# Output parts moved on ScalarE, X^T parts queued behind them, and W loaded elsewhere in a fused long-convolution and score kernel

## The chip, the cores and the metric

The kernel runs on one core of one Trainium2 chip. A core has a matrix engine (TensorE, PE in the profile; its weight loads, which overlap the matmuls, are PEld), three engines for elementwise work (VectorE or DVE, ScalarE or ACT, GpSimd or POOL), and a queue engine (SyncE or SP), which issues the transfers between the device's memory and the core's on-chip memory. Sixteen DMA engines carry out all transfers. The metric is the device time of one execution in microseconds (us); less is better.

## The reference

The input x has 4 images of 64 channels of 256 x 256. Two layers follow. The first filters every channel with a kernel of its own: `k = hx[i] * hy[j]`, an outer product of two vectors that a small network with sines makes, so the two-dimensional convolution is two one-dimensional ones.

```python
y = irfft2(rfft2(x, 512 x 512) * rfft2(k) / 512)[:256, :256]
x = y + x * bias[channel]
```

The second layer weighs each image's matrix of row products, adds the sum of each row to the row, and normalizes each channel over all images:

```python
scores = einsum('bpsd,bptd->bpst', x, x) / sqrt(256)
y = x + sum(scores * weights, axis=-1, keepdims=True)
y_hat = (y - mean(y)) * rsqrt(var(y) + 1e-5)     # over images, rows, columns
out = y_hat * gamma + beta
```

## The kernel before, in words

Everything is float32. The kernel goes through the 64 channels one by one; all four images of a channel are worked on together, as two pairs v = 0, 1. Each convolution is a product with a Toeplitz matrix, which is read from a table in device memory with overlapping rows. A channel passes through several stages, and different stages of different channels overlap. One turn c of the main loop (L545 to L592) contains:

- On TensorE, always in this order: `conv_x0(c)` (L233), the second convolution of channel c; `conv_z(c + 1)` (L210), the first one of the next channel; `gram(c, 0)` and `gram(c, 1)` (L270), the row products of the two pairs. This text calls one such turn on TensorE a block, and its phase is the time since its first conv_x0 matmul.
- On VectorE: `x0` (L240), which takes the convolution's result out of the accumulators and adds x times bias; `weigh` and `spread` (L290, L294, L304), which multiply the row products by W; `add_red` (L326), which adds the row sums to x0 of channel p = c - 1; and five small instructions of `scale_shift` (L386 to L394).
- On GpSimd: `all_sum` (L312), a sum over partitions of 1,024 columns, and two short sums (L330, L372).
- On ScalarE: `copy_h(c + 1)` (L192) doubles the Toeplitz rows of the next channel, which conv_z(c + 1) needs; `minus_mean` and `squares` (L361, L362, L366) of channel q = c - 2; `copy_z` (L219), four copies out of accumulators for the next block's conv_x0; `pick_red` (L319), which moves half of the row sums and which add_red waits for; `root` (L378 to L382), three tiny instructions; and four output parts.

An output part is `finish(g, sh, v, n)` (L399): ScalarE computes x0 times g plus sh for half n of pair v (L406, 128 x 512 elements), and SyncE writes the result o out (L407, 256 KB). The four parts of a channel are written (0,0), (0,1), (1,0), (1,1) in this text. Parts (0,0) and (0,1) of channel f = c - 3 come at the end of turn c; parts (1,0) and (1,1) follow in the next turn, where the channel is called e = c - 4.

The order on each engine is the order in which the program is written (`manual_schedule`, L83): nothing reorders it. All loads of the loop and all writes stand on SyncE's one queue, also in written order. An entry that has to wait holds up those behind it. A turn loads X^T of channel c + 3 in four parts of 256 KB (L72, four buffers for each pair), W of channel c + 1 (L78, 320 KB, two buffers), and the Toeplitz rows of channel c + 2 in four groups of 36 KB (L187, three buffers). Before the change a turn's queue on SyncE is: W; rows 0; part (1,0); rows 1; X^T (0,0); part (1,1); rows 2; X^T (1,0); part (0,0); rows 3; X^T (0,1); part (0,1); X^T (1,1). W's load waits until VectorE has used the W of channel c - 1 for the last time (L294).

The last two channels are written out on their own (`last_channels`, L439). It takes over the open output parts of the loop.

Of the kernel before, what the change touches and what calls it, by code (L numbers as in the profile page):

```python
# [15 lines left out]
B, C, S = 4, 64, 256  # L16
# [21 lines left out]
def conv_scores_bn_kernel(  # L38
# [29 lines left out]
    def load_xt(c, v, n):  # L68
        if not n:
            xts[c, v] = ld.tile([P, 4, S], F32, tag=f"xt{v}", name=f"xt_{c}_{v}", bufs=4)  # L70
        part = bass.ts(n, 2)
        nc.sync.dma_start(xts[c, v][:, part], xT[c, v, :, part])  # L72
# [3 lines left out]
    def load_w(c):  # L76
        w = ld.tile([P, 10, H], F32, tag="w", name=f"w_{c}", bufs=2)
        nc.sync.dma_start(w, wl[c])  # L78
        ws[c] = w
# [97 lines left out]
    def load_h(c, n):  # L177


        if not n:  # L180
            hs[c] = ld.tile([P, 2, GW], F32, tag="toep", name=f"toep_{c}")
        src = bass.AP(
            g_dram.tensor, g_dram.offset + c * 2 * GW + 16 * n,
            [[4 + C * 2 * GW, COPIES], [1, 4], [1, GW + S]],
        )
        rows = hs[c][bass.ts(n, 16)].rearrange("p a r -> p (a r)")
        nc.sync.dma_start(rows[:, : GW + S], src)  # L187

    def copy_h(c):

        toep = hs[c]
        nc.scalar.copy(toep[H:, :, :S], toep[:H, :, :S])  # L192
# [7 lines left out]
    def conv_z(c, m):  # L200


        toep = hs[c]
        p1 = [ps.tile([P, 2, S], F32, tag="ps", name=f"p1_{c}_{m}_{u}") for u in range(2)]
        for k in range(2):
            for i in range(4):
                for t in range(4):
                    u, v = t % 2, t // 2
                    rows = bass.ts(u, H)
                    nc.tensor.matmul(  # L210
                        p1[u][bass.ts(v, H), k, : S - H * i],
                        lhsT=xts[c, v][rows, i, bass.ts(2 * m + k, H)],
                        rhs=toep[rows, 1, H * i : S], start=(i == 0), stop=(i == 3),
                    )
        return p1

    def copy_z(c, m, p1):
        for u in range(2):
            nc.scalar.copy(zs[c][:, u, bass.ts(m, 2), :], p1[u][:, :, ::-1])  # L219

    def conv_x0(c, z, parts=range(2)):


        xt = [xts[c, v] for v in range(2)]
        toep, x0 = hs[c], st8[c][0]
        for m in parts:
            p2 = [ps.tile([P, 2, S], F32, tag="ps", name=f"p2_{c}_{m}_{v}") for v in range(2)]
            for i in range(2):
                for k in range(4):
                    for t in range(4):  # L230
                        v, u = t % 2, t // 2
                        rows = bass.ts(v, H)
                        nc.tensor.matmul(  # L233
                            p2[v][bass.ts(u, H), i, : S - H * k],
                            lhsT=z[rows, u, k, bass.ts(2 * m + i, H)],
                            rhs=toep[rows, 0, H * k : S], start=(k == 0), stop=(k == 3),
                        )
            for v in range(2):
                part = bass.ts(m, 2)
                nc.vector.scalar_tensor_tensor(  # L240
                    x0[:, v, part], xt[v][:, part], chan_sb[:, 0, c : c + 1],
                    p2[v][:, :, ::-1], ALU.mult, ALU.add,
                )
# [195 lines left out]
    def last_channels(c):  # L439


        p, q, f, e = c - 1, c - 2, c - 3, c - 4


        begin(p)
        copy_h(c)
        conv_x0(p, zs.pop(p))
        load_w(c)
        minus_mean(moms[f])
        squares(f, moms[f], 0)  # L450
        finish(*fins[e - 1], 1, 0)
        squares(f, moms[f], 1)
        tot = sum_squares(f, moms[f])
        fins[e] = (e, *scale_shift(e, moms[e], *scales[e]))
        begin_z(c)
        copy_z(c, 0, conv_z(c, 0))
        finish(*fins[e - 1], 1, 1)
        mom_q = sm.tile([P, 8], F32, tag="mom", name=f"mom_{q}")
        rps = [red_by_pe(q, v) for v in range(2)]
        for v in range(2):  # L460
            add_red_of(q, v, rps[v], mom_q)
        nc.gpsimd.partition_all_reduce(mom_q[:, 2:4], mom_q[:, 0:2], P, RED.add)
        scales[f] = root(f, tot)
        copy_z(c, 1, conv_z(c, 1))
        finish(*fins[e], 0, 0)
        finish(*fins[e], 0, 1)
        fins[f] = (f, *scale_shift(f, moms[f], *scales[f]))
        gram(p, 0)


        begin(c)
        minus_mean(mom_q)
        squares(q, mom_q, 0)
        squares(q, mom_q, 1)
        tot = sum_squares(q, mom_q)
        z = zs.pop(c)
        conv_x0(c, z, [0])
        mom_p = sm.tile([P, 8], F32, tag="mom", name=f"mom_{p}")
        add_red_of(p, 0, red_by_pe(p, 0), mom_p)
        conv_x0(c, z, [1])  # L480
        finish(*fins[e], 1, 0)
        finish(*fins[e], 1, 1)
        scales[q] = root(q, tot)
        fins[q] = (q, *scale_shift(q, mom_q, *scales[q]))
        finish(*fins[f], 0, 0)
        finish(*fins[f], 0, 1)
        first_mean(mom_p)
        squares(p, mom_p, 0)
        gram(p, 1)
        finish(*fins[f], 1, 0)  # L490
        finish(*fins[f], 1, 1)
        for n in range(2):
            finish(*fins[q], 0, n)
        gram(c, 0, weighed=False)
        rp = red_by_pe(p, 1)
        for u in range(2):
            weigh(c, u, banks.pop(0))
        add_red_of(p, 1, rp, mom_p)
        sums_p = sum_second(p, mom_p)
        squares(p, mom_p, 1)  # L500
        nc.gpsimd.partition_all_reduce(sums_p[:, 2:4], mom_p[:, 6:8], P, RED.add)
        for n in range(2):
            finish(*fins[q], 1, n)
        gram(c, 1, weighed=False)
        mom = sm.tile([P, 8], F32, tag="mom", name=f"mom_{c}")
        add_red_of(c, 0, red_by_pe(c, 0), mom)
        first_mean(mom)
        for u in range(2):
            weigh(c, 2 + u, banks.pop(0))
        rp = red_by_pe(c, 1)  # L510
        drift(mom_p, sums_p)
        scales[p] = root_of_rest(p, sums_p)
        add_red_of(c, 1, rp, mom)
        sums = sum_second(c, mom)
        squares(c, mom, 0)
        squares(c, mom, 1)
        nc.gpsimd.partition_all_reduce(sums[:, 2:4], mom[:, 6:8], P, RED.add)
        fins[p] = (p, *scale_shift(p, mom_p, *scales[p]))
        drift(mom, sums)
        finish(*fins[p], 0, 0)  # L520
        finish(*fins[p], 0, 1, vector=True)
        scales[c] = root_of_rest(c, sums)
        finish(*fins[p], 1, 0)
        finish(*fins[p], 1, 1)
        fins[c] = (c, *scale_shift(c, mom, *scales[c]))
        for v in range(2):
            finish(*fins[c], v, 0)
            finish(*fins[c], v, 1, vector=True)
# [16 lines left out]
    for c in range(C - 2):  # L545
        p, q, f, e = c - 1, c - 2, c - 3, c - 4
        begin(c)
        copy_h(c + 1)
        conv_x0(c, zs.pop(c))

        load_w(c + 1)
        load_h(c + 2, 0)
        if q >= 0:
            minus_mean(moms[q])
            squares(q, moms[q], 0)
        if e >= 0:
            finish(*fins[e], 1, 0)
        load_h(c + 2, 1)
        if c + 3 < C:
            load_xt(c + 3, 0, 0)  # L560
        if q >= 0:
            squares(q, moms[q], 1)
            tot = sum_squares(q, moms[q])
        if f >= 0:
            fins[f] = (f, *scale_shift(f, moms.pop(f), *scales.pop(f)))
        begin_z(c + 1)
        copy_z(c + 1, 0, conv_z(c + 1, 0))
        if e >= 0:
            finish(*fins.pop(e), 1, 1)
        load_h(c + 2, 2)  # L570
        if c + 3 < C:
            load_xt(c + 3, 1, 0)
        copy_z(c + 1, 1, conv_z(c + 1, 1))
        if f >= 0:
            finish(*fins[f], 0, 0)
        load_h(c + 2, 3)
        if c + 3 < C:
            load_xt(c + 3, 0, 1)
        if p >= 0:
            pick_red(p)  # L580
        if q >= 0:
            scales[q] = root(q, tot)
        if f >= 0:
            finish(*fins[f], 0, 1)
        if c + 3 < C:
            load_xt(c + 3, 1, 1)
        gram(c, 0)
        if p >= 0:
            moms[p] = add_red(p)
        gram(c, 1)  # L590
        if c < BY_PE:
            all_sum(c)  # L592
    last_channels(C - 1)


# [67 lines left out]
```

## Time and profile before

| What | Value |
|---|---|
| Time, median of 3 runs | 881.24 us (880.01 to 884.09) |
| Profiled execution, its own time | 883.99 us |
| Span of that execution | 882.2 us |
| Granted TensorE clock, mean | 0.992 |
| TensorE busy | 860.4 us, 98% |
| VectorE busy | 754.9 us, 86% |
| ScalarE busy | 616.7 us, 70% |
| GpSimd busy | 425.1 us, 48% |
| Moved by DMA | 169.68 MB, mean 192 GB/s |

A row of the groups in the profile gives the line, the engine, the operation, what it writes and reads, and then the busy time and the mean of one instruction. Rows of waits read "engine line waited for: us in total, times, longest us". An arrow points at what ended the wait; "issue" stands there where the engine waited for nothing that the profile shows. A row of the timeline gives start, duration, engine, line and, in brackets, the engine's idle time just before it. Start times count from the span's start. q1 is the DMA queue of SyncE; q8 carries packets of instructions for the engines.

### The profile page before, as it was taken

What the parts mean: (1) busy time and instruction counts of PE and PEld (TensorE: products, weight loads), DVE (VectorE), ACT (ScalarE), POOL (GpSimd) and SP (SyncE); (2) the same over time, 40 slices, a digit from 0 to 9 for tenths busy, and PEclk for the clock granted to TensorE, in tenths of its full rate; (3) what the DMA queues carried; (4) which work ended last, traced back from release to release, by engine and by line L of the source; (5) the groups of instructions that cost most, each with busy time, mean ns of one, the idle gap of its engine ahead of it and who ended that gap; (6) DMA issues with size and microseconds to landing.
All of it is one profiled execution on the core that took longest, in us unless ns stands there. A gap on an engine that the chain in (4) does not pass through costs nothing.

```text
span 882.2 us, 55900 instructions
## 1 busy us (share of the span) xinstructions
PE 860.4 (98%) x24678; PEld 827.0 (94%) x24678; DVE 754.9 (86%) x2642; ACT 616.7 (70%) x1212; POOL 425.1 (48%) x195
## 2 busy tenths in 40 slices
PE   7999999999999999999999999999999999999993
PEld 5999999999999999999999999999999999999992
DVE  3588988998898898898898898898898898898885
ACT  2257767767777777776776776776776776776784
POOL 0236446546545545645645644645645545645600
PEclk9999999999999999999999999999999999999996
DMA  6525556556556556556556565556556556556534
GB/s 187 178 88 176 198 197 211 198 190 212 198 196 212 192 199 208 197 194 211 192 199 209 197 197 202 196 193 207 191 192 210 183 201 206 201 193 206 182 124 169
DMA packets 89913, 169.68 MB, mean 192 GB/s; under 512 B 10566, under 2 KB 11784, under 8 KB 89672
## 3 DMA queue, kind: packets, MB, share of 16 engines
q1 hardware_dynamic: 89116, 165.51, 55.5%
q8 instruction: 194, 3.18, 1.5%
q10 hardware_dynamic: 556, 0.61, 0.2%
q14 instruction: 47, 0.39, 0.1%
HBM read 98.18 MB, written 67.76 MB: 188 GB/s over the span
## 4 chain that ended last, share of the span: by engine, by line
PE 97%; DVE 1%; ACT 0%; issue 0%; DMA 0%; ACTq 0%; SPq 0%; DVEq 0%
PE p L210 32%; PE p L233 32%; PE g L270 32%; PE rp L341 0%; PE rp L346 0%; PE idle L167 0%; DVE x L355 0%; DMA fb_sb<-in_fb 0%; ACT o L406 0%; PE ph L147 0%; PE ph L131 0%; DVE fa L134 0%; DVE fa L139 0%; DVE junk L290 0%; ACT z L219 0%
## 5 line engine op out<-in xcount | busy, mean ns | idle before, releaser
L312 POOL PARTITION_ALL_REDUCE rd<-sp x61 | 373.5, 6122 | 183.8 <-DVE sp L304 183.8
L233 PE MATMUL p<-toep,z 64*64 64x256 f32 (+3 forms) x8192 | 300.6, 296 | 1.2 <-issue 1.0
L210 PE MATMUL p<-toep,xt 64*64 64x256 f32 (+3 forms) x8192 | 299.8, 296 | 0.4 <-issue 0.2
L233 PEld LDWEIGHTS p<-toep,z 64*64 64x64 f32 x8192 | 285.5, 133 | 14.4 <-issue 2.8
L270 PE MATMUL g<-x 64*64 64x192 f32 (+1 forms) x8192 | 298.1, 296 | 0.4 <-issue 0.3
L210 PEld LDWEIGHTS p<-toep,xt 64*64 64x64 f32 x8192 | 282.9, 133 | 12.2 <-PE idle L167 0.7
L270 PEld LDWEIGHTS g<-x 64*64 64x64 f32 x8192 | 283.3, 133 | 2.8 <-issue 1.0
L290 DVE SCALAR_TENSOR_TENSOR junk<-g,w 128x192 f32<-128x192 f32 x512 | 161.1, 352 | 86.5 <-PE g L270 86.5
L406 ACT ACTIVATE o<-x,sh,g 128x512 f32<-128x512 f32 x253 | 203.5, 808 | 0.0
L240 DVE SCALAR_TENSOR_TENSOR x<-xt,chan_sb,p 128x512 f32<-128x512 f32 x256 | 174.1, 742 | 9.0 <-PE p L233 9.0
L219 ACT COPY z<-p 128x512 f32<-128x512 f32 x256 | 134.7, 577 | 31.1 <-PE p L210 31.1
L366 ACT ACTIVATE sq<-x,mom 128x1024 f32<-128x1024 f32 x128 | 146.3, 1143 | 5.4 <-DVE x L355 2.0
L326 DVE SCALAR_TENSOR_TENSOR x<-x,rd 128x1024 f32<-128x1024 f32 x122 | 144.2, 1220 | 0.1
L304 DVE SCALAR_TENSOR_TENSOR sp<-eye_sb,red,pr 128x128 f32<-128x128 f32 x488 | 138.1, 346 | 0.0
L330 POOL PARTITION_ALL_REDUCE mom<-mom x61 | 24.3, 399 | 235.0 <-DVE x L326 230.9
L294 DVE SCALAR_TENSOR_TENSOR pr<-g,w 128x256 f32<-128x256 f32 x256 | 107.5, 420 | 0.0
L319 ACT COPY rd<-rd 64x512 f32<-64x512 f32 x61 | 37.6, 616 | 91.1 <-POOL rd L312 91.1
L361 ACT ACTIVATE mom<-mom 128x1 f32<-128x1 f32 x62 | 18.3, 295 | 77.3 <-POOL mom L330 77.3
L192 ACT COPY toep<-toep 64x512 f32<-64x512 f32 x63 | 38.9, 617 | 39.9 <-DMA toep<-g_dram 26.4
L290 DVE DVE_READ_ACCUMULATOR junk<-g,w 128x1 f32 x512 | 42.6, 83 | 0.0
L372 POOL PARTITION_ALL_REDUCE tot<-mom x62 | 29.7, 480 | 9.5 <-ACT sq L366 9.5
L366 ACT ACTIVATION_READ_ACCUMULATOR sq<-x,mom 128x1 f32 x128 | 23.8, 186 | 0.0
(60 smaller groups left out, 212.0 us busy)
## 6 DMA issues: line engine op xcount, KB each, us to landing
xt<-in_xT SPq DMA_DIRECT2D x256, 256.0 KB
out<-o SPq DMA_DIRECT2D x256, 256.0 KB
w<-in_wl SPq DMA_DIRECT2D x64, 320.0 KB
toep<-g_dram SPq DMA_DIRECT2D x252, 36.0 KB
g_dram<-g_sb SPq DMA_DIRECT2D x1, 320.0 KB
g_dram<-g_sb ACTq DMA_DIRECT2D x1, 320.0 KB
decay_sb<-in_decay SPq DMA_DIRECT2D x1, 256.0 KB
fw_sb<-in_fw ACTq DMA_DIRECT2D x1, 192.0 KB
```

Source lines behind the costliest of these rows:

```text
L210: nc.tensor.matmul(p1[u][bass.ts(v, H), k, : S - H * i], lhsT=xts[c, v][rows, i, bass.ts(2 * m + k, H)], rhs=toep[rows, 1, H * i : S], sta ...
L219: nc.scalar.copy(zs[c][:, u, bass.ts(m, 2), :], p1[u][:, :, ::-1])
L233: nc.tensor.matmul(p2[v][bass.ts(u, H), i, : S - H * k], lhsT=z[rows, u, k, bass.ts(2 * m + i, H)], rhs=toep[rows, 0, H * k : S], start=(k ...
L240: nc.vector.scalar_tensor_tensor(x0[:, v, part], xt[v][:, part], chan_sb[:, 0, c : c + 1], p2[v][:, :, ::-1], ALU.mult, ALU.add,)
L270: nc.tensor.matmul(gs[u][bass.ts(h, H), o, :], lhsT=xb[rows, v, i, m, :], rhs=xb[rows, v, i, t, :], start=(i == 0), stop=(i == 3),)
L290: nc.vector.scalar_tensor_tensor(junk, g[:, part, :], 1.0 / math.sqrt(S), w[:, 3 * n : 3 * n + 3, :], ALU.mult, ALU.mult, accum_out=red0[: ...
L294: nc.vector.scalar_tensor_tensor(pr[:, b].rearrange("p (t s) -> p t s", s=H), g[:, COL, :], 1.0 / math.sqrt(S), w[:, 6:10, :], ALU.mult, A ...
L304: nc.vector.scalar_tensor_tensor(sp[:, b, part], eye_sb, red0[:, b, n : n + 1], pr[:, b, part], ALU.mult, ALU.add,)
L312: nc.gpsimd.partition_all_reduce(rd.rearrange("p b s -> p (b s)"), sp.rearrange("p b s -> p (b s)"), P, RED.add)
L326: nc.vector.scalar_tensor_tensor(x0[:, v], x0[:, v], 1.0, rd[:, 2 * v, None, :].to_broadcast([P, 4, S]), ALU.mult, ALU.add, accum_out=mom[ ...
L366: nc.scalar.activation(sq, st8[c][0][:, v], AF.Square, bias=mom[:, 5:6], accum_out=mom[:, 6 + v : 7 + v])
L406: nc.scalar.activation(o, y, AF.Identity, bias=sh, scale=g)
```

## The change

The amount of work is unchanged; every instruction and every transfer of before is there after. Moved are:

- `pick_red(p)` on ScalarE from behind part (0,0) to ahead of it.
- Part (0,1) of the output from the end of a turn to the next turn, behind `copy_h`. In the last channels the open part (0,1) of channel 58 goes to the same place.
- On SyncE's queue, the X^T parts: each now follows an output part. X^T (0,0) goes ahead of rows 1, X^T (0,1) follows part (0,0) directly, and the last one, X^T (1,1), goes with part (0,1) into the next turn, where it is loaded for channel c + 2.
- W of channel c + 1 from the head of the queue to behind X^T (1,0), ahead of rows 3.

A turn's queue on SyncE after the change is: part (0,1); X^T (1,1); rows 0; part (1,0); X^T (0,0); rows 1; part (1,1); rows 2; X^T (1,0); W; rows 3; part (0,0); X^T (0,1).

```diff
@@ last_channels
         begin(p)
         copy_h(c)
+        finish(*fins[e - 1], 0, 1)
         conv_x0(p, zs.pop(p))
         load_w(c)
@@ main loop
         begin(c)
         copy_h(c + 1)
+        if e >= 0:
+            finish(*fins[e], 0, 1)
+        if c + 2 < C and c:
+            load_xt(c + 2, 1, 1)
+        load_h(c + 2, 0)
         conv_x0(c, zs.pop(c))
-
-        load_w(c + 1)
-        load_h(c + 2, 0)
         if q >= 0:
             minus_mean(moms[q])
             squares(q, moms[q], 0)
         if e >= 0:
             finish(*fins[e], 1, 0)
-        load_h(c + 2, 1)
         if c + 3 < C:
             load_xt(c + 3, 0, 0)
+        load_h(c + 2, 1)
         if q >= 0:
             squares(q, moms[q], 1)
             tot = sum_squares(q, moms[q])
...
         load_h(c + 2, 2)
         if c + 3 < C:
             load_xt(c + 3, 1, 0)
+        load_w(c + 1)
+        load_h(c + 2, 3)
         copy_z(c + 1, 1, conv_z(c + 1, 1))
+        if p >= 0:
+            pick_red(p)
         if f >= 0:
             finish(*fins[f], 0, 0)
-        load_h(c + 2, 3)
         if c + 3 < C:
             load_xt(c + 3, 0, 1)
-        if p >= 0:
-            pick_red(p)
         if q >= 0:
             scales[q] = root(q, tot)
-        if f >= 0:
-            finish(*fins[f], 0, 1)
-        if c + 3 < C:
-            load_xt(c + 3, 1, 1)
         gram(c, 0)
```

## The prediction

> **What bounds the kernel now.** I read the page first (busy shares, then the chain that ended last), then the waits, then one block on ScalarE and SyncE in the timeline.
>
> ```profile
> span 882.2 us, 55900 instructions
> ...
> PE 860.4 (98%) x24678; PEld 827.0 (94%) x24678; DVE 754.9 (86%) x2642; ACT 616.7 (70%) x1212; POOL 425.1 (48%) x195
> ...
> q8 instruction: 194, 3.18, 1.5%
> ```
>
> TensorE is busy for 98% of the span, and 97% of the chain of waits lies on it. The stretch 16.7 to 850.7 us of the loop has 831.99 us of TensorE in 834.00. The chain shows the three parts of a channel, L233 (conv_x0), L210 (conv_z) and L270 (gram), with 4.36, 4.37 and 4.35 us. A channel's block thus takes 13.08 us, and most blocks take exactly that. Next, the waits of the engines and of the DMA queue:
>
> ```profile
> ACT rd L319 <- POOL rd L312: 91.1, 60, 2.3
> ...
> ACT mom L361 <- POOL mom L330: 77.3, 60, 5.6
> ...
> ACT toep L192 <- DMA toep<-g_dram: 26.4, 34, 2.4
> ACT toep L192 <- issue: 13.2, 19, 1.7
> ...
> PEld p L233 <- issue: 2.8, 6, 1.1
> ...
> PEld g L270 <- issue: 1.0, 3, 0.4
> ```
>
> ScalarE waits in three places of a block, together (91.1 + 77.3 + 26.4 + 13.2)/60 = 3.5 us, and none of them holds up TensorE. SyncE's queue waits 169.1 us in 62 times for VectorE before it can load W, and 202.9 us for output parts. TensorE's only loop waits are of kind "issue": nothing in the program releases them. The chain shows one, the largest:
>
> ```profile
> 679.92 1.64 PE p L233 x32
> 681.56 0.71 issue
> 682.27 1.75 PE p L233 x27
> ```
>
> From the starts of the L233 groups I took the length of every block. After the first, eleven loop blocks exceed 13.08 us, and their excess sums to 4.8 us. The weight load after each gap above 0.25 us stands at the same place of TensorE's instruction stream, counted modulo 256, and an instruction packet (queue q8, 194 of them, 16 KB each) ends 1.3 to 1.5 us before it. So these are waits for instructions. Laying packet k beside the time at which TensorE passed the boundary before it shows that each is asked for one boundary ahead, 4.36 us early. From request to end it takes 2.04 us in the mean. It stalls TensorE when that passes about 4.36 - 1.35 = 3.0 us. That happens when data fill the DMA engines: requests at 10.5 to 11.5 us of a block, behind the long burst of transfers, take 2.7 to 3.1 us in the mean, those at 5.0 to 5.5, in the pause, 1.4.
>
> [...]
>
> **The change, part by part.** I lay block 441.54 to 454.62 out anew (phases count from its start; a phase over 13.08 belongs to the next block).
>
> ```profile
> 440.87 0.61 ACT L319 COPY rd<-rd 64x512 f32<-64x512 f32 x1 [1.57 <-POOL rd L312]
> ...
> 442.22 0.80 ACT L406 ACTIVATE o<-x,sh,g 128x512 f32<-128x512 f32 x1
> 443.79 0.62 ACT L192 COPY toep<-toep 64x512 f32<-64x512 f32 x1 [0.77 <-issue]
> 445.40 0.29 ACT L361 ACTIVATE mom<-mom 128x1 f32<-128x1 f32 x1 [0.99 <-POOL mom L330]
> ```
>
> *pick_red ahead of part (0,0).* It waits for GpSimd's sum, which ends at 440.9 whatever ScalarE does, so it starts when it did; its idle time grows from 1.57 to 2.37. Queued behind it: part (0,0), root and copy_h. Part (0,0) (0.80) and root (0.74) end at 441.48 + 1.54 = 443.02, where root and part (0,1) ended before: copy_h can start as early as it did. VectorE's add_red takes pick_red's result at 442.43, as before. Root is 0.8 later, at 443.0; VectorE reads it at 450.18. Cost 0. Were GpSimd late, all five would be late as they were before.
>
> *Part (0,1) behind copy_h.* copy_h waits for its fourth row group until 443.79 and ends at 444.41. The part runs to 445.21, in the idle 0.99 us before 445.40. Cover left: 0.19 us. Where copy_h is later (2.8 us into the block at worst, against 2.25 here), the part pushes the squares by up to 0.4 us, then the copies of z; those end at phase 10.0 and TensorE wants them at 13.08. Cost 0; without that 3 us it would be 0.4 us in some blocks. In the last channels one part moves the same way, in the same cover.
>
> *W.* It leaves the place where it blocked SyncE from phase 1.9 to 5.06 and goes behind the third X^T part, issued at about 10.8, for a use one block later. Its buffer is freed by phase 5. It removes 2.7 us of queue wait a block, but SyncE bounds nothing: the same transfers now wait for output parts instead. Cost 0.
>
> *X^T and Toeplitz parts.* The X^T part moved into the next block is used 17 us after its issue. The fourth row group was issued at 11.35, behind 804 KB since 9.30, and landed at phase 1.6 of the next block on average. Now it goes at 11.2 behind 868 KB: 64 KB more are 0.2 us, some 1.8. TensorE needs copy_h done by 4.36, so it may land at 3.7. Cost 0.
>
> *The instruction packets.* This is the one term that can move. KB by start of issue, before: 512 from phase 1.5, 904 in 5.1 to 7.6, 1,096 in 9.3 to 12.0. After: 512 from 0.8 (part (0,0), X^T), 548 from about 3, 548 from 6.5, 904 in 9.3 to 11.2 (part, rows, X^T, W, rows), then nothing until 13.9. The sum is the same 2,512 KB. The longest burst shrinks by 192 KB, 0.55 us at the 348 GB/s that half a microsecond of full DMA shows, and the second splits. But the longest is now denser, 904 KB in 1.9 us where 804 came in 2.05. A stall needs only one packet requested within some 0.5 us behind a burst, and a 512 KB pair did it too: a request at phase 2.35, just behind a pair, waited 2.56 us to start. Adding up both schedules as one first-in-first-out queue that drains at 250 GB/s gives a mean backlog at the requests of 0.56 us before and 0.59 after, no difference that I would trust: such a sum follows the measured waits of before only loosely (correlation 0.36). So the bounds of this term are -4.8 us (all stalls gone) and about +5 (the slower rival). I take -0.7.
>
> Sum against the profiled execution, 883.99 us = 882.2 span + 1.8 around it: TensorE's work unchanged, 0 from ScalarE, VectorE and SyncE, -0.7 from packets. That execution stalls more than the median of the runs shown: without its 4.8 us it would be 879.2, and the runs shown are 880.01, 881.24 and 884.09. The median run therefore holds some 2.0 us of stalls, of which I take 0.7 off: 880.5 us.
>
> **The rivals.** *Smooth queue:* no stall is left. For it: the pause in the queue is kept, and longest bursts shrink. Against: stalls behind 512 KB pairs. It gives 879.2, or 878.5 if profiling itself costs a little: still within half a per cent of 881.24, and only an unseen extra of 2 us or more would make it faster.
>
> *Dense burst (the slower side):* part (1,1), X^T and W stand back to back from 9.3 to 10.8, and packets requested there wait behind them. In the built order of the changed kernel TensorE's stream has 5 extra wait instructions a block (6 before), so a request's phase drifts by 5/768 x 13.08 = 0.085 us a block, and stays in a bad window 1 us wide for 12 blocks. Requests at 10.5 to 11.5 already take 2.7 to 3.1 us. A further 64 KB and denser arrival add 0.2 to 0.4. That is 12 x 0.4 = 5 us beyond the median run, 886. It decides once requests of that window take over 3.0 us as a rule.
>
> *Late copy_h:* the row group lands after phase 3.7, and TensorE waits at L210 in every block; each 0.1 us costs 6 us. Against: 1.8 us of cover. *Nothing happens* is contained in the forecast: TensorE's work is the same.
>
> **How the numbers follow.** Forecast (stalls of about the same size, 879.5 to 883.5) 0.62; smooth queue 0.23, of it 0.05 under 876.8; dense burst 0.12, of it 0.10 over 885.6; late copy_h 0.03, all over 885.6. Half a per cent is 4.4 us, about what a measurement of this kernel can tell from no change, so those two bounds are 876.8 and 885.6. Faster is 0.05; slower 0.10 + 0.03 = 0.13; same 0.62 + 0.18 + 0.02 = 0.82. The range may leave 2 in 10 out: it goes from 878.0, a little under the smooth queue's 878.5, to 885.6, where the dense burst's larger part begins.
>
> **What would show it.** Right: TensorE at 860 us busy; most blocks 13.08 us; ScalarE's wait for rd grown to some 2.3 us, its wait for mom shrunk to a few tenths; SyncE no longer waiting for pr; "issue" waits of PEld of 2 to 6 us in the loop. Wrong: a PEld or PE wait at L210 for ScalarE's copy, or a dozen neighbouring blocks with gaps of half a microsecond.

## The result, and the profile after

The changed kernel takes 879.44 us (median of 22 runs, 877.74 to 881.58), the kernel before, run again beside it, 883.63 us (22 runs, 880.01 to 890.20). The ratio is 0.9944, with a 95% interval of 0.9930 to 0.9959: 0.56% faster. The three runs of before that were known at first had a median of 881.24 us; the larger set shows that this was a low draw. The spread shrank as well, from 10.2 us to 3.8. All medians in this document hold every run; the ratios leave out runs that took over 1.5% longer than the fastest run of the same kernel.

The page of the changed kernel, busy times and the queue of instruction packets:

```profile
span 877.3 us, 55962 instructions
...
PE 857.4 (98%) x24678; PEld 836.7 (95%) x24678; DVE 754.9 (86%) x2642; ACT 620.6 (71%) x1212; POOL 425.1 (48%) x195
...
q8 instruction: 194, 3.18, 1.5%
```

The engines do the same work; the trace has 62 instructions more, all of them semaphore instructions (among them 120 more on SyncE, and 331 instead of 387 on TensorE). The span is 4.9 us shorter. Where it went is seen in the waits of the changed kernel:

```profile
ACT rd L319 <- POOL rd L312: 135.9, 60, 2.4
...
ACT mom L361 <- POOL mom L330: 35.0, 49, 5.9
...
ACT toep L192 <- DMA toep<-g_dram: 24.2, 37, 3.4
...
ACT toep L192 <- issue: 6.1, 13, 1.1
...
PEld g L270 <- issue: 0.4, 2, 0.2
...
PEld p L210 <- ACT toep L192: 0.3, 1, 0.3
...
PEld p L233 <- issue: 0.2, 1, 0.2
PEld p L210 <- issue: 0.2, 1, 0.2
```

The weight loads' waits of kind "issue" were 2.8 and 1.0 us at L233 and L270, as the prediction shows, and at L210 in the kernel before:

```profile
PEld p L210 <- issue: 0.5, 2, 0.3
```

Now they are 0.2, 0.4 and 0.2. The one wait for ScalarE's copy (0.3 us, at L210) is in the first block. From the starts of the blocks: after the first, their excess over 13.08 us sums to 0.66 us in the changed kernel and to 4.78 us before. That is 4.1 of the span's 4.9 us. The other 0.8 lies ahead of the loop, where nothing was changed: the first conv_z matmul starts at 15.96 us instead of 16.74, so it is no part of the change's effect. The two profiles are single executions: that of before took 883.99 us, that of the changed kernel 879.23, both near their medians. The loop of the changed kernel now looks like this in the chain, block after block:

```profile
453.54 4.31 PE p L233 x87
457.84 0.05 PE p L210
457.90 4.31 PE p L210 x86
462.21 0.05 PE g L270
462.27 4.24 PE g L270 x120
```

On ScalarE one block of the changed kernel reads (brackets: idle time before the instruction):

```profile
439.59 0.61 ACT L319 COPY rd<-rd 64x512 f32<-64x512 f32 x1 [2.29 <-POOL rd L312]
440.23 0.81 ACT L406 ACTIVATE o<-x,sh,g 128x512 f32<-128x512 f32 x1
...
441.76 0.62 ACT L192 COPY toep<-toep 64x512 f32<-64x512 f32 x1
442.41 0.81 ACT L406 ACTIVATE o<-x,sh,g 128x512 f32<-128x512 f32 x1
444.12 0.29 ACT L361 ACTIVATE mom<-mom 128x1 f32<-128x1 f32 x1 [0.90 <-POOL mom L330]
```

Part (0,0) follows pick_red, part (0,1) follows copy_h, and both end before ScalarE has to wait for the mean's sum, as laid out in the prediction.

### The profile page after: what moved, and what is told of

Read it like the earlier page. It is cut to its first block, busy times and chain, and to the rows that moved or that the text cites. A ratio compares the mean times of both kernels' runs of the same rounds, so it can differ in the third digit from the quotient of the medians.

```text
span 877.3 us, 55962 instructions
## 1 busy us (share of the span) xinstructions
PE 857.4 (98%) x24678; PEld 836.7 (95%) x24678; DVE 754.9 (86%) x2642; ACT 620.6 (71%) x1212; POOL 425.1 (48%) x195
## 4 chain that ended last, share of the span: by engine, by line
PE 97%; DVE 1%; DMA 1%; ACT 0%; issue 0%; ACTq 0%; DVEq 0%
PE p L210 32%; PE g L270 32%; PE p L233 32%; PE rp L341 1%; PE rp L346 0%; DMA toep<-g_sb 0%; PE ph L131 0%; DVE x L355 0%; ACT o L406 0%; DMA fw_sb<-in_fw 0%; DVE fa L134 0%; DVE fa L139 0%; ACT z L219 0%; ACT fh L141 0%; DVE fk L138 0%
## 5 line engine op out<-in xcount | busy, mean ns | idle before, releaser
L233 PE MATMUL p<-toep,z 64*64 64x256 f32 (+3 forms) x8192 | 301.8, 296 | 0.1
L210 PE MATMUL p<-toep,xt 64*64 64x256 f32 (+3 forms) x8192 | 301.7, 296 | 0.1
L270 PE MATMUL g<-x 64*64 64x192 f32 (+1 forms) x8192 | 300.4, 296 | 0.1
L233 PEld LDWEIGHTS p<-toep,z 64*64 64x64 f32 x8192 | 292.5, 133 | 7.2 <-ACT z L219 0.6
L210 PEld LDWEIGHTS p<-toep,xt 64*64 64x64 f32 x8192 | 289.4, 133 | 7.4 <-PE idle L167 0.7
L270 PEld LDWEIGHTS g<-x 64*64 64x64 f32 x8192 | 287.6, 133 | 0.7 <-issue 0.4
L319 ACT COPY rd<-rd 64x512 f32<-64x512 f32 x61 | 37.5, 615 | 135.9 <-POOL rd L312 135.9
```

Source lines behind the costliest of these rows:

```text
L210: nc.tensor.matmul(p1[u][bass.ts(v, H), k, : S - H * i], lhsT=xts[c, v][rows, i, bass.ts(2 * m + k, H)], rhs=toep[rows, 1, H * i : S], sta ...
L233: nc.tensor.matmul(p2[v][bass.ts(u, H), i, : S - H * k], lhsT=z[rows, u, k, bass.ts(2 * m + i, H)], rhs=toep[rows, 0, H * k : S], start=(k ...
L270: nc.tensor.matmul(gs[u][bass.ts(h, H), o, :], lhsT=xb[rows, v, i, m, :], rhs=xb[rows, v, i, t, :], start=(i == 0), stop=(i == 3),)
```

## The experiments

A *packet* is one of the 194 transfers of 16,384 bytes on q8, which took 0.88 to 2.45 us each in the profile of before. TensorE's stream there has 49,746 instructions (24,678 weight loads, as many matmuls, 390 others), 256.4 for each packet; hence the count modulo 256. A packet counts as asked for when TensorE passes the boundary 256 instructions ahead. That is a reading of the starts, as in the prediction: of the 172 packets of the fifth to 61st block none began more than 0.2 us ahead of that moment; the mean came 1.0 us after it, the last 2.9. The 3.0 us from request to end, over which a packet counts as long below, are the prediction's estimate, 4.36 us between boundaries less 1.35 us between a packet's end and its first weight load.

Three theories stood against each other. *Fetch:* what a block takes beyond 13.08 us is TensorE waiting for packets of instructions, which are late when they are asked for behind much data on the DMA engines; the change spreads the data. *ScalarE:* the gain is in the new order of pick_red and the parts. *Queue:* the gain is that W no longer blocks SyncE. Late copy_h was kept as a fourth.

One thing must be known to read the results: the kernel before took different times in the four groups of runs. Each later group ran on one chip at one time, so chip and time cannot be told apart, and the chip of the first pair is not on record; this text says "chip" for a group. Each group has the kernel before beside it. It was profiled in the first group only.

| Kernel | us | Before, same chip | Ratio (95%) | Gaps at place 194 | Other gaps |
|---|---|---|---|---|---|
| before, first chip | 883.63 | | | 10, 4.5 us | none |
| changed kernel, first chip | 879.44 | 883.63 | 0.9944 (0.9930 to 0.9959) | 2, 0.4 us | none |
| W moved only | 907.29 | 895.88 | 1.0128 (1.0072 to 1.0185) | 33, 19.1 us | 16, 4.9 us |
| all but W | 884.26 | 895.88 | 0.9884 (0.9845 to 0.9923) | 7, 3.4 us | none |
| pick_red moved only | 898.59 | 895.88 | 0.9990 (0.9963 to 1.0017) | 46, 24.9 us | 9, 2.6 us |
| before without X^T loads | 879.71 | 895.88 | 0.9830 (0.9788 to 0.9872) | 3, 0.8 us | none |
| one burst | 932.29 | 885.60 | 1.0497 (1.0457 to 1.0537) | 51, 46.8 us | 6, 0.9 us |
| before, shifted | 884.91 | 885.60 | 0.9988 (0.9969 to 1.0007) | 19, 9.3 us | none |
| changed, shifted | 879.87 | 885.60 | 0.9928 (0.9905 to 0.9950) | 5, 1.5 us | none |
| W in halves, two pauses | 883.58 | 885.60 | 0.9975 (0.9962 to 0.9988) | 14, 5.2 us | none |
| W in halves, in place | 884.28 | 891.90 | 0.9912 (0.9880 to 0.9944) | 7, 2.1 us | none |
| W behind X^T (0,1) | 894.88 | 891.90 | 1.0023 (0.9996 to 1.0051) | 29, 15.5 us | 1, 0.2 us |
| changed kernel again | 884.05 | 891.90 | 0.9899 (0.9855 to 0.9942) | 5, 1.3 us | 10, 3.6 us |
| all but W again | 883.28 | 891.90 | 0.9890 (0.9848 to 0.9932) | 11, 4.5 us | none |

The last two columns come from the profiled execution, which need not be the median one: gaps of over 0.23 us between the starts of two weight loads from the second block to the 62nd, with the usual 0.11 us taken off each. "Place 194" means that the weight load after the gap stands within two instructions of place 194 of TensorE's stream, counted modulo 256. The count starts at the trace's first TensorE instruction, so the number 194 itself means nothing; that it is the same everywhere does. Smaller waits are not in these columns. For "pick_red moved only" the profiled execution is the slowest of 22, 910.04 us, and its blocks exceed 13.08 us by 30.9 us in all, 3.4 more than the columns hold; for "changed kernel again" it is the slowest of six, and for "W in halves, in place" the fastest of ten.

**Does the data on the DMA engines cause the stalls?** Take the X^T loads of channels 4 and up away (old tiles are used again, so the output is another function's) and leave every engine's work as it is:

```diff
     def load_xt(c, v, n):
+        if c >= 4:
+            xts[c, v] = xts[c - 4, v]
+            return
         if not n:
```

> The kernel before without the X^T loads of channels 4 and up, which reuse the tiles of channels 0 to 3 (the output is then another function's); all engines do the same work in the same order. Fetch theory: bursts of at most 648 KB, almost no stalls, 878 to 880 us, ratio 0.993 to 0.996, blocks at 13.08 us. ScalarE and queue theory: nothing changes, 1.000.

879.71 us, where the kernel before takes 895.88. A stretch of its loop, as the window view shows it (busy time of PE, PEld, DVE, ACT, POOL, then clock, DMA share, GB/s):

```profile
16.00:846.00 830.00, 829.82 (x24266) 790.06 (x24268) 726.54 (x2535) 591.69 (x1167) 422.14 (x184) 1.00 0.35 118
```

With the order of the rest of SyncE's queue, ScalarE's order and W's place unchanged, 16.2 us are gone (895.88 to 879.71). SyncE even waits longer for W's buffer than in the profile of before (215.4 us against 169.1). So these 16 us are a matter of data moved, and no engine's order has to change to remove them. The fetch theory holds; the ScalarE and queue theories, which expected no change, fall as sole causes. The time also shows the floor: 879 to 880 us, where the changed kernel is on the first chip.

The opposite: all X^T parts and W in one run, with the changed kernel's ScalarE order kept.

```diff
-        if c + 2 < C and c:
-            load_xt(c + 2, 1, 1)
...
-        if c + 3 < C:
-            load_xt(c + 3, 0, 0)
...
         load_h(c + 2, 2)
-        if c + 3 < C:
-            load_xt(c + 3, 1, 0)
-        load_w(c + 1)
         load_h(c + 2, 3)
+        if c + 3 < C:
+            for part in PARTS:
+                load_xt(c + 3, *part)
+        load_w(c + 1)
...
-        if c + 3 < C:
-            load_xt(c + 3, 0, 1)
```

> The changed kernel, its ScalarE order kept, with all four X^T parts and W in one run behind part (1,1) and the rows: 1,672 KB from phase 9.3. Fetch theory: instruction packets requested behind that burst are late in many blocks, slower than the kernel before, ratio 1.005 to 1.03, and the gaps of the weight loads stand at place 194 of the stream modulo 256. ScalarE theory: the gain stays, ratio as that of the changed kernel.

932.29 us, 5.0% slower than before; the direction was expected, the size not. The waits of its weight loads:

```profile
PEld p L210 <- issue: 41.5, 40, 2.1
PEld p L233 <- issue: 4.1, 6, 2.0
```

At L210 these are forty gaps of a microsecond on average, "issue" all of them. 51 of the 57 gaps stand at place 194. The same bytes are moved as in the changed kernel and ScalarE's order is the same; only the distribution of the loads differs, and the two are 5.7% apart (1.0497/0.9928, the latter from the shifted changed kernel on the same chip).

**Is it really the instruction stream, and was the phase lucky?** Ahead of the loop three warming matmuls were replaced by 32 small ones, 116 more instructions in the stream, in both kernels.

```diff
-        for n in range(3):
-            idle = fps.tile([P, 3, P], F32, tag="idle", name=f"idle_{n}", bufs=1)
-            nc.tensor.matmul(idle, lhsT=fw_sb[:, 3, :], rhs=fw_sb[:, 1:, :], start=True, stop=True)
+        idle = [
+            fps.tile([P, 8, H], F32, tag="idle", name="idle_0", bufs=1),
+            fps.tile([P, 2, H], F32, tag="ph", name="idle_1"),
+        ]
+        for n in range(32):
+            u, v, o = n % 2, n // 2 % 2, n // 4
+            rows = bass.ts(u, H)
+            nc.tensor.matmul(
+                idle[u][bass.ts(v, H), o % (2 if u else 8), :],
+                lhsT=fw_sb[rows, 3, :H], rhs=fw_sb[rows, 1, :H], start=True, stop=True,
+            )
```

> The kernel before with the three warming matmuls ahead of the loop replaced by 32 small ones: 116 more TensorE instructions ahead of the loop, so each packet boundary lies 116/768 x 13.08 = 2.0 us earlier in a block. Fetch theory: the gaps still stand at place 194 modulo 256 of the stream, now at other matmuls of a block, and their sum is like before's: ratio 0.995 to 1.005. Theory that the phase was bad luck: half of the stalls or fewer, ratio 0.99 on a chip where before stalls by 16 us.

> The changed kernel with the same shift of 116 instructions. Fetch theory through bursts: 879 to 881 us as without the shift. Theory that the changed kernel only met a lucky phase: several us of stalls more, 883 to 890.

Both came as the fetch theory expected: 884.91 us against 885.60 for the kernel before, 879.87 for the changed one. In the shifted kernel before, all 19 gaps stand at place 194 of the lengthened stream. Its chain shows the largest (L241 and L218 are conv_x0 and conv_z there):

```profile
684.99 1.25 PE p L241 x32
686.25 1.51 issue
687.76 0.56 PE p L241 x13
```

A cause that sat in the matmuls themselves, such as a late operand, would have stayed with the matmul; the gaps moved with the count of instructions. The changed kernel's gain stays under this second phase, so it is not the luck of one.

**Which part of the change brings it?** W's move alone:

```diff
         conv_x0(c, zs.pop(c))
-        load_w(c + 1)
         load_h(c + 2, 0)
...
             load_xt(c + 3, 1, 0)
+        load_w(c + 1)
         copy_z(c + 1, 1, conv_z(c + 1, 1))
```

> The kernel before with only W's load moved behind X^T (1,0). Fetch theory (what is lost over 13.08 us a block is waiting for instruction packets behind bursts of data): W leaves the second burst and joins the longest one, 1,096 + 320 = 1,416 KB from phase 9.3 to 12.4, so there is no gain, ratio to before 1.000 to 1.006, issue waits of the weight loads as before or more. Queue theory (the gain is that W no longer blocks SyncE): most of the gain is here, ratio 0.995. ScalarE theory (the gain is in its new order): 1.000.

It is 1.3% slower, twice the fetch theory's bound and opposite to the queue theory: SyncE's wait for W's buffer falls to some 41 us, and the kernel loses.

```profile
PEld p L233 <- issue: 13.8, 22, 1.6
...
PEld p L210 <- issue: 3.3, 6, 1.3
PEld p L210 <- ACT toep L192: 3.0, 10, 0.4
```

Most of it is late packets (33 gaps at place 194, 19.1 us), as W joins the longest burst (1,416 KB). Its 16 other gaps, which the fetch theory did not count on, lie at the beginning of conv_z (L210): there rows 3, queued behind W, landed too late for copy_h. pick_red's move alone:

```diff
         copy_z(c + 1, 1, conv_z(c + 1, 1))
+        if p >= 0:
+            pick_red(p)
         if f >= 0:
             finish(*fins[f], 0, 0)
         load_h(c + 2, 3)
...
-        if p >= 0:
-            pick_red(p)
```

> The kernel before with only pick_red ahead of part (0,0). Part (0,0) then ends 1.9 us later and the fourth Toeplitz rows, behind it on the queue, are issued at phase 14.3 and land at about 4.0 to 4.6 of the next block. Late copy_h theory: TensorE waits at L210 for ScalarE's copy, 0.3 to 0.9 us a block, 900 to 935 us in all. ScalarE theory: ratio 0.995.

No gain: the ratio is 0.9990, the median of all 22 runs lies 2.7 us above that of before, and both theories missed. Late copy_h was expected to cost 0.3 to 0.9 us in every block. In ten blocks of the profile, from 293 us on, rows 3 landed at phase 2.6 to 4.5, and in the whole loop only 9 gaps of 2.6 us in all are of that kind; most of this slowest execution's stalls are packets. So pick_red's new place is worth nothing by itself. Part (0,1) on ScalarE was not moved alone.

Everything but W:

```diff
             load_xt(c + 2, 1, 1)
+        load_w(c + 1)
         load_h(c + 2, 0)
...
-        load_w(c + 1)
         load_h(c + 2, 3)
```

> The changed kernel with W back ahead of rows 0, where SyncE waits for it until phase 5. Fetch theory: bursts of 512, 904 (W, rows, part, X^T, rows) and 584 KB, the longest shorter than before's 1,096; some gain, ratio 0.995 to 0.998. Queue theory: the gain is gone, 1.000. ScalarE theory: the whole gain stays, 0.9944.

0.9884, a larger gain than any theory gave; their numbers came from the first chip, where before stalls less. The queue theory, under which the gain should be gone, falls. The ScalarE theory would fit here, but not in the two experiments with the loads removed and put in one burst. Run again beside the changed kernel on one chip:

> The changed kernel with W ahead of rows 0 again, now beside the changed kernel on one chip. Its time beyond the changed kernel is what W's place is worth once the rest is made: 2 to 5 us, from 884.3 us against 879.4 on two chips.

> The changed kernel once more, to stand on the same chip as the two others and the next: 879 to 881 us, few issue waits in the loop, whatever the kernel before takes on this chip.

883.28 us without W's move, 884.05 with it: no difference (the intervals of the ratios overlap almost wholly), where 2 to 5 us were expected. The gain is in the output parts and X^T together, which no run separates; W's new place is then as good as the old one, and without them it is harmful. The table hints at why the two are equal: in their profiled executions the new place has fewer late packets (1.3 us of gaps against 4.5) but 3.6 us of other gaps, where the old has none.

The repeated changed kernel was expected at 879 to 881 us whatever the chip, and took 884.05. Its profiled execution, the slowest of its runs (886.71 us), shows much of why. The waits of its weight loads and of ScalarE's copy, and one such copy:

```profile
ACT toep L192 <- DMA toep<-g_dram: 50.1, 44, 4.0
...
ACT toep L192 <- issue: 14.4, 14, 3.4
...
PEld p L210 <- ACT toep L192: 2.6, 8, 0.5
```

```profile
184.44 0.62 ACT L192 COPY toep<-toep 64x512 f32<-64x512 f32 x1 [3.61 <-DMA toep<-g_dram]
```

In seven blocks in a row, from 166 us on, rows 3 landed at phase 3.4 to 4.3 and copy_h started at 3.8 to 5.1; TensorE waited for it in most of them. That is the late copy_h of the prediction, present on this chip and absent from the loop in the profile of the first. The new order can carry it on from block to block: part (0,1), now behind copy_h, heads the turn's queue on SyncE, and in these blocks rows 3 had been issued at phase 12.9 to 14.2 of the block before where the median is 11.7. No run tests this.

**Is it the longest burst, or the pause behind it?** W in two halves, in two pauses, makes the longest burst 708 KB instead of 904.

```diff
+        half_w(c + 1, 0)
         if q >= 0:
             squares(q, moms[q], 1)
...
-        load_w(c + 1)
         load_h(c + 2, 3)
...
             load_xt(c + 3, 0, 1)
+        half_w(c + 1, 1)
```

> The changed kernel with W in two halves of 160 KB, one behind rows 1, one behind X^T (0,1): bursts of 672, 548, 708 and 584 KB instead of 512, 548, 548 and 904. Fetch theory: the last stalls, at requests behind the 904 KB, go: 878 to 879.5 us, 0 to 1 us under the changed kernel, blocks of 13.08 us without exception.

It was expected to be the better kernel and is not: 883.58 us, where the shifted changed kernel takes 879.87 on that chip (the unshifted one did not run there). So the length of the longest burst alone does not decide. Two explanations were left, the halves' shorter rows of 1,280 bytes, or the filled pauses. The halves back to back in W's place:

```diff
         w = ld.tile([P, 10, H], F32, tag="w", name=f"w_{c}", bufs=2)
-        nc.sync.dma_start(w, wl[c])
+        for half in range(2):
+            part = bass.ts(half, 5)
+            nc.sync.dma_start(w[:, part], wl[c][:, part])
```

> The changed kernel with W in two halves of 160 KB, back to back at the place where the whole one stands, ahead of rows 3. If rows of 1,280 bytes (q1's share of the DMA engines was 56.9% with halves, 55.1% with the whole W) are what slowed the kernel with halves in two pauses: as slow as that one, 3 to 4 us over the changed kernel. If its filled pauses were: within 1 us of the changed kernel.

884.28 against the changed kernel's 884.05: shorter rows cost nothing that shows. And the whole W in another pause:

```diff
-        load_w(c + 1)
         load_h(c + 2, 3)
...
             load_xt(c + 3, 0, 1)
+        load_w(c + 1)
```

> The changed kernel with the whole W behind X^T (0,1), at phase 1.7, where the next part follows at about 3: bursts of 832, 548, 548 and 584 KB, the longest shorter than the changed kernel's 904, but no pause behind it. If the longest burst decides: as fast as the changed kernel or up to 1 us faster. If the pause behind a burst decides: 2 to 6 us slower than the changed kernel.

894.88 us, 10.8 over the changed kernel, more than the 2 to 6 expected. Its longest burst is 832 KB, shorter than 904, but the next 548 KB follow W within about 1.3 us. In its profile, packets asked for at phase 2.0 to 2.5 take 3.57 us in the mean from request to end (seven packets), where the changed kernel on that chip has 2.20 (six); 35 packets are over 3.0 us, against 13.

This fits the account that a burst does harm when more is queued before the DMA engines have caught up. The account can be held against the traces by counting the bytes that SyncE has issued and q1 has not yet moved. They are over 500 KB for 20% of the loop here and for 12% in the changed kernel beside it. For the halves in two pauses the same count shows no difference: 8%, against 9% in the shifted changed kernel, though its packets take 2.31 us from request to end in the mean, against 1.95. And all but W, where W's burst is followed by a pause of only 1.0 us, is as fast as the changed kernel. So the count agrees with the account for W behind X^T (0,1), and what slows the halves stays open. None of these variants beats the changed kernel.

## Why the prediction was right or wrong

**The bound** was right. TensorE's matmuls set the time, a block is 13.08 us, and in the kernel before what the loop takes beyond it is waiting for packets. The shift of the stream and the removal of X^T show this; in the prediction it was only argued from the trace.

**pick_red, part (0,1), W, at 0 each:** right on the first chip. ScalarE's wait for rd grew from 1.5 to 135.9/60 = 2.27 us a block (2.3 predicted). Its wait for mom shrank to 35.0/60 = 0.58 us (a few tenths predicted). SyncE's wait for W's buffer, first before, then after:

```profile
SPq L78 <- DVE pr L294: 169.1, 62, 10.3
```

```profile
SPq L78 <- DVE pr L294: 30.9, 11, 10.4
...
SPq L78 <- DVE junk L290: 9.9, 16, 1.0
```

The prediction expected none to be left; what is left lies mostly in the first turns. The row group, put at 1.8, landed at 1.55 in the mean and at 2.5 at the latest. One reading was off: copy_h starts 3.4 us into the block at worst in the profile of before, not 2.8; in the changed kernel it is 2.9. On the last chip the row group's cover of 1.8 us was used up in some blocks, so "cost 0" holds for the first chip, not for every one.

**The instruction packets, at -0.7 us:** that this term is the one that moves, and downwards, was right; its size was off. The term measured -4.1 us in the profiles (4.78 to 0.66) and -4.2 in the medians (883.63 to 879.44): nearly its lower bound of -4.8, the smooth queue. The sign "issue waits of 2 to 6 us" accordingly failed: they are 0.8 us at the three loop lines. Two things made the term small. The sum over both schedules as one queue showed no difference between them (0.56 and 0.59 us; its drain of 250 GB/s was an estimate, beside 253 and 264 GB/s in two busy stretches of 2 us of the profile of before, and no run shows a queue of that kind), and I let that weigh although it followed the measured waits only loosely. And the base was low: I took the median run to hold 2.0 us of stalls, from three runs; over 22 runs it holds 883.63 - 879.2 = 4.4.

The traces say that the sum was not wrong about the amount: at the packets' requests, the bytes issued and not yet moved are 287 KB in the mean before and 285 after (fifth to 61st block). Yet the packets over 3.0 us fell from 15 of 172 to 3. So the mean amount ahead of a request is not what the change improves. That data on the DMA engines make packets late is shown (51 gaps at place 194, 46.8 us, with the loads in one burst; 3, 0.8 us, without X^T's); which property of the new order makes the longest waits rarer stays open.

**The time** of 880.5 us (878.0 to 885.6) was met, at 1.1 us off, and that is luck: the base was 2.4 us too low and the gain 3.5 us too small, and the two errors nearly cancel. **The sign** was not well judged: 0.05 for faster by more than half a per cent, and 0.56% came, with an interval from 0.41 to 0.70 that holds half a per cent too. With 883.63 as the base, the smooth queue's 879.2 would have been just at that bound, so its share of 0.23 would have been split there.

**The dense burst** did not come: in the changed kernel requests at 11.0 to 11.5 take 2.75 us in the mean (five packets), which is under the 3.0 named as the point of decision, and three packets of 172 are over it. But a longer burst is a true danger: W's move alone, with 1,416 KB in it, is 1.3% slower.

## What to carry to other kernels

When TensorE is 98% busy and still short of its own pace, look at gaps of kind "issue" and count the instructions between them. A common place modulo 256 meant late instruction packets here (10 gaps, 4.5 us, in the kernel before). With TensorE's work as it was, 3 gaps and 0.8 us stood there without the X^T loads, and 2 and 0.4 us in the changed kernel. Do not judge a schedule by its longest burst alone: a shorter longest burst with the pauses filled was slower twice (708 KB: 883.58 us against 879.87; 832 KB: 894.88 against 884.05, where the changed kernel's is 904 KB), and one large load moved without the others was too (907.29 against 895.88). Look at what else a moved load now stands in front of; W ahead of rows 3, moved alone, made copy_h late (TensorE waited for it ten times, 3.0 us). Measure such a change with more than three runs and beside the old kernel each time, because the old kernel's time differed between the groups of runs (883.6 to 895.9 us).

## What the runs showed that was not expected

The kernel before takes 883.6, 895.9, 885.6 and 891.9 us in the four groups, although the most frequent block is of 13.08 us in every profile that was taken; without the X^T loads it is at 879.7 us in the second. What that group takes longer, 16.2 us of it, is therefore in stalls that depend on the loads; for the others this was not tried. Why the same schedule is served later in one group than in another was not tried either.

In nearly every gap at place 194 the first weight load of a packet started 1.2 to 1.6 us after the packet's end (1.3 to 1.6 in the ten gaps of the kernel before), in kernels as different as the one with a single burst and the one without X^T. A request waited up to 4.1 us to start in the one-burst kernel, against 2.9 in the kernel before and 2.3 in the changed one.
